# x loaded back beside the edge statistics, and column copies from step 6 to 16 steps before the end, in a graph message-passing kernel on one core

## The chip, the core and the metric

The kernel runs on one core of a Trainium2 chip. Its engines have queues of their own and meet at semaphores: TensorE (PE, weight loads listed as PEld), VectorE (DVE), ScalarE (ACT), GpSimd (POOL) and SyncE (SP), which here issues most of the DMA transfers. The metric is the device time of one execution in microseconds (us). The time before is the median of three runs.

## The reference, cut to what matters

A graph of 12,500 nodes with 96 features and 412,500 directed edges sorted by their target node (a self loop for each node among them). For each edge the rows of x at its source and at its target and a vector made from four edge attributes are joined and put through a linear layer, ReLU and a normalization over all edges (a batch norm); the messages are summed by target node, the nodes' own branch and x are added, and every row is normalized.

```python
def _mlp(h, W, b, gamma, beta):
    h = relu(h @ W + b)
    mu = mean(h, axis=0); var = mean(square(h - mu), axis=0)
    return gamma * (h - mu) * rsqrt(var + EPS) + beta

node_feat = _mlp(x, W_node, ...)
edge_feat = _mlp(edge_attr, W_edge, ...)
message   = _mlp(concat([x[src], x[dst], edge_feat], axis=1), W_msg, ...)
agg       = segment_sum(message, dst, num_segments=12500)
out       = layernorm(x + agg + node_feat)
```

Since the edge features' normalization needs the statistics of all edges, a first pass over the edge attributes comes ahead of the messages.

## The kernel before, in words

**Stages, in order of time.** (1) `tables`: x, transposed, lies in SBUF as `big` (96 partitions, one column of four bytes a node). From it the kernel makes two tables in DRAM, `p_tab` (x times the source part of the message weights) and `q_tab` (the target part). (2) Small things, and `nodes`: the node branch, which overwrites `big` with x plus node branch, and stores that, projected, in `y0_d`. (3) `edge_norm`, the edge statistics: 26 iterations, each with three loads of edge attributes (`ea`, L379), 24 matmuls (L385), 12 ReLUs on ACT (L389) and 24 statistics on DVE (L391). (4) the message stage in `fast`. (5) `output`.

**Gathers.** 412,500 edges are cut into tiles of 128, four tiles make a group (512 edges, 806 groups), four groups a block. For each tile POOL issues an indirect DMA that fetches 128 rows of `p_tab` (L226, `gather`). A ring of seven tiles, each for a pair of groups, holds what was gathered ahead: 14 groups. Since POOL would have nothing to do in stages 1 to 3, the first 116 groups (29 blocks) are gathered then and stored to a DRAM buffer (`spill`, the generator `blocks`, called `store`): each `next(store)` issues 16 gathers on POOL and, on SP, the store of the block two back. They come back 768 KB at a time (`pb`, `fetch`) in the message stage. The first four of these blocks are gathered as raw rows of x before the tables exist, and `convert` multiplies them by the weights in the message stage, group by group, with PE, ACT, PE and DVE in turn.

**The message stage.** `plan` gives an order of the 202 blocks, in which a spilled block follows every five or six others, and from it the steps: one group a step, 806 in all. The order of the instructions of SP, POOL, PE, DVE and ACT is written out by hand (`manual_schedule`). At step k, for group g: every fourth step SP issues the loads of the block two ahead (`load`, `fetch`); `message` on DVE adds the gathered rows to the linear part in PSUM and applies ReLU (L615 for the tiles gathered, L618 and L621 for the fourth tile of some groups); on odd steps ACT squares two groups (L634) and DVE sums squares (L640); `sums` on PE adds up by place (L666); `edges` and `prepare` make the left operand of a coming block (L588, L596); `linear` on PE makes the linear part two steps ahead (L602); and POOL gathers the group 14 ahead (`ahead_of`).

**What relieves POOL.** The fourth tile of some groups isn't gathered. For 40 groups SP fetches its rows one by one, 16 transfers of 384 bytes every second step over 16 steps, with row numbers read into SP's registers (`apart_rows`, `rows_of`, L433); three spilled groups get theirs so in stage 3 (`early_rows`). For others, the *columns*, DVE and ACT copy 128 single columns of x from `big` into a tile `xc` of 96 x 128 (72 copies on DVE, L745, 56 on ACT, L747), from addresses in registers, which are loaded from a small tile of numbers (`clin`, L716, by SP; L733 the register load); `linear` multiplies `xc` by the source weights and adds it to the linear part (L606). Copies are laid out in slots, three in two steps (`XS`); a column takes four slots (`XN`), so 18 copies on DVE and 14 on ACT a slot on average. The slots begin at step `XA`; a column goes to the first group at least four steps after its last slot that has no such help yet and lies ahead of a margin at the end of the stage:

```python
for slot in range(XA // 2 * XS, len(steps) // 2 * XS, XN):
    done = (slot + XN - 1) // XS * 2 + 1
    free = [g for s, g in steps[done + 4:len(steps) - 24] if g >= SPILL and g not in rows and g not in columns]
```

**x for the columns.** Since `nodes` overwrote `big`, x is loaded again, in 14 pieces of 336 KB on SP's queue: `piece`, L697, one on each even step from 2 to 28. After the last copy, `residual` loads `y0_d` into `big` for the output (L453), one load a step from two to three steps past the last slot on.

Of the kernel before, what the change touches and what calls it, by code (L numbers as in the profile page):

```python
# [23 lines left out]
N, C, E, ED = 12500, 96, 412500, 4  # L24
EPS = 1e-5
P = 128
# [16 lines left out]
NB = -(-N // P)  # L43
NN = NB * P
NBK = 4
CH = 14
# [9 lines left out]
SPILL = 29 * BG  # L56
# [12 lines left out]
SR, SS = 16, 2  # L69
SG, SF = 4 * BG, SPILL + 24  # L70
SB = 22
XA, XS, XN = 34, 3, 4
XACT = 56
ROW = 4 * C
FIRST = 16512
# [14 lines left out]
def plan():  # L90

    early, late = list(range(SPILL // BG)), list(range(SPILL // BG, NBL))
    order = []
    for i, b in enumerate(late):
        order.append(b)
        while early and (SPILL // BG - len(early)) * (len(late) - LEAD - SPACE) < (i - LEAD) * (SPILL // BG):
            order.append(early.pop(0))
    assert not early
    steps = [(s, g) for s, b in enumerate(order) for g in range(b * BG, min((b + 1) * BG, NG))]
    at_step = {g: k for k, (s, g) in enumerate(steps)}  # L100
    rows = {g: at_step[g] - SB - at_step[g] % 2 for g in FETCHED[len(EARLY):]}
    columns = {}
    for slot in range(XA // 2 * XS, len(steps) // 2 * XS, XN):
        done = (slot + XN - 1) // XS * 2 + 1
        free = [g for s, g in steps[done + 4:len(steps) - 24] if g >= SPILL and g not in rows and g not in columns]
        if free:
            columns[free[0]] = slot
    return order, steps, rows, columns
# [6 lines left out]
def gnn(ctx, tc, t):  # L115
    nc = tc.nc
    big = ctx.enter_context(tc.tile_pool(name="big", bufs=1)).tile([P, NN], F32, name="big")
# [17 lines left out]
    xp = big[:C]  # L135
    nc.scalar.dma_start(w_msg, t["L0_gnn_W_msg"].rearrange("(s k) f -> k s f", k=C))
    for i in range(0, NB, CH // 2):
        part = slice(i * P, min(i + CH // 2, NB) * P)
# [133 lines left out]
    for i in range(NS):  # L272
        k, n = Q * i, C - Q * i
# [176 lines left out]
    def residual(i):  # L450
# [3 lines left out]
        return y  # L454

    order, steps, by_row, by_column = plan()

    def fast(ring):
# [8 lines left out]
        with tc.manual_schedule(engines={ET.SP, ET.Pool}):  # L467
            nc.sync.dma_start(q_tab[:WM, :], zero[:WM])
            for r in range(WM + NN, WT, 64):
                n = min(64, WT - r)  # L470
                nc.sync.dma_start(q_tab[r:r + n, :], zero[:n])
            for i in range(2):
                next(store)
            places()
            for i in range(3):
                next(store)
            for i, _ in enumerate(nodes()):
                if i in (1, 4, 9):
                    next(store)
            n, extra = 10, early_rows()  # L480
            for i, _ in enumerate(edge_norm()):
                if i:
                    next(extra, None)
                while 14 * i + 180 >= 20 * n:
                    next(store, None)
                    n += 1
            for _ in store:
                pass
            for _ in extra:
                pass  # L490
            got = {g: ahead_of(g) for g in range(SPILL, SPILL + RING)}
        with tc.tile_pool(name="fix", bufs=1) as fix, tc.tile_pool(name="msg", bufs=2) as work, \
# [196 lines left out]
            apart, numbers, held = {}, {}, {}  # L689
            row_start = {k: (i + len(EARLY), g) for i, (g, k) in enumerate(by_row.items())}  # L690
            column_start = {k: g for g, k in by_column.items()}
            pieces = list(range(0, NB, CH // 2))
            loads = list(range(-(-NB // NBY)))

            def piece(i):
                to = slice(i * P, min(i + CH // 2, NB) * P)
                nc.sync.dma_start(big[:C, to], t["xp"][:, to])  # L697

            def apart_rows(k):

# [49 lines left out]
            n, ahead = len(steps), SPILL + RING  # L750
            row_numbers(lin, len(EARLY))
            with tc.manual_schedule(engines={ET.SP, ET.Pool, ET.PE, ET.DVE, ET.Activation}):
                bad = nc.values_load(flag, min_val=0, max_val=1, skip_runtime_bounds_check_because="a comparison's result")
                load(0)
                fetch(0)
                load(1)
                fetch(1)
                for half in range(2):
                    edges(0, half)
                    prepare(0, half)  # L760
                edges(1, 0)
                for k in range(ZB - 1):
                    linear(k)
                places_of(0)
                waiting, last = None, BG * (len(order) - 1)
                for k in range(last):
                    s, g = steps[k]
                    if g % BG == 0:
                        if s + 2 < len(order):
                            load(s + 2)  # L770
                            fetch(s + 2)
                    if k % 2 == 0 and k and pieces:
                        piece(pieces.pop(0))
                    apart_numbers(k)
                    if k % 2 == 0:
                        load_numbers(k, 0, ET.DVE)
                    message(k)
                    load_numbers(k, 1, ET.DVE) if k % 2 else copy_columns(k, 0, ET.DVE)
                    j = k - LATER - BG - 1
                    if k % 2:  # L780
                        load_numbers(k, 1, ET.Activation)
                        copy_columns(k, 1, ET.Activation)
                        now = squared(k - 1)
                        load_numbers(k, 2, ET.Activation)
                        copy_columns(k, 1, ET.DVE)
                        if waiting:
                            moments(waiting, k == last - 1, lambda: load_numbers(k, 2, ET.DVE))
                        waiting = now
                        copy_columns(k, 2, ET.DVE)
                        copy_columns(k, 2, ET.Activation)  # L790
                    if g % BG == 3 and s + 1 < len(order):
                        places_of(s + 1)
                    if j >= 0 and j % BG == 0:
                        add(j // BG, place(j // BG))
                    if k >= LATER:
                        sums(k - LATER)
                    if g % BG != 3 and s + 1 < len(order):
                        if g % 2:
                            edges(s + 1, 1)
                        else:  # L800
                            prepare(s + 1, g % BG // 2)
                    if g % BG == 3:
                        if s + 1 < len(order) and order[s + 1] < RAW:
                            convert(s + 1)
                        if s + 2 < len(order):
                            edges(s + 2, 0)
                    if k + ZB - 1 < n:
                        linear(k + ZB - 1)
                    if k % 2 == 0:
                        load_numbers(k, 0, ET.Activation)  # L810
                        copy_columns(k, 0, ET.Activation)
                    if g >= SPILL:
                        got[ahead] = ahead_of(ahead)
                        ahead += 1
                    apart_rows(k)
                    if k >= (max(column_start) + XN) // XS * 2 + 3 and loads:
                        y0s.append(residual(loads.pop(0)))
                assert not apart and not loads and not pieces

                s, g = len(order) - 1, steps[last][1]  # L820
                m, r = NT - (g + 1) * GT, E - (NT - 1) * P
                collect(waiting.rearrange("p g t c -> p (g t c)"), 2 * GT)
                message(last)
                sq = [squared(last, 1, GT)]
                sums(last - 2)
                sums(last - 1)
                unread(BUSY - 1)
                message(n - 1)
                sq.append(squared(n - 1, 1, m))
                collect(sq[0][:, 0, :, :].rearrange("p t c -> p (t c)"), GT)  # L830
                sums(last)
                at_end = place(s - 1), place(s)
                unread(1)
                collect(sq[1][:, 0, :, :].rearrange("p t c -> p (t c)"), m, r)
                add(s - 1, at_end[0])
                sums(n - 1)
                unread(1)
                square_sum = by_place[s % 2][:C, P:P + 1]
                nc.tensor.matmul(square_sum, squares, ones, start=True, stop=True)
                unread(BUSY)  # L840
                mean_square = fix.tile([C, 1], F32, name="mean_square")
                add(s, at_end[1])
                nc.vector.tensor_scalar(mean_square, square_sum, 1.0 / E, None, op0=OP.mult)
# [236 lines left out]
```

## Time and profile before

| | |
|---|---|
| time, median of 3 runs | 5507.97 us (5506.36 to 5508.45) |
| the profiled execution's own time | 5517.2 us |
| its span | 5515.5 us |
| granted TensorE clock, mean | 0.624 |
| instructions | 97011 |
| edge statistics, first matmul to last statistics | 362.4 to about 942 us |
| first message to last message (806 steps) | 986.9 to 5470.0 us |
| column copies, first to last | 1183 to 5363 us |
| gathers | 2901 |

Rows of groups give the line, the engine and the operation, out<-in by the program's names, the count, then busy time in us and mean ns of one, then the idle time of the engine just before them and what ended most of it. "issue" means that the engine waited for nothing the profile shows. Rows of a timeline give the start, the duration, engine (SPq is SP's queue), line, operation and count, and the idle time before. Rows of stretches give begin and end, length, the busy time and count (x) of the instructions chosen, the granted clock, the share of the DMA engines and GB/s. Rows of waits give who waited for whom: us in total, times, longest. Rows of a line's instructions give shortest, median and longest ns, and the first and last start in us.

### The profile page before, as it was taken

How to read it: one execution, taken by the hardware profiler on the slowest of the kernel's cores; microseconds unless marked ns; L12 is line 12 of the kernel's file. 1: busy time of each engine (PE TensorE's matmuls, PEld its weight loads, DVE VectorE, ACT ScalarE, POOL GpSimd, SP SyncE). 2: the span in 40 equal slices, each digit the busy share in tenths (PEclk: the TensorE clock that was granted, in tenths of full speed). 3: DMA queues.
4: the chain of work that ended last, by engine and by line, in shares of the span. 5: the costliest groups of instructions: out<-in, count | busy, mean ns of one | idle time of the engine just before them, and what ended most of it. 6: DMA issues, size and time to landing. Idle time of an engine off the chain costs nothing. (4 is left out here: it accounts for less than half of the span.)

```text
span 5515.5 us, 97011 instructions
## 1 busy us (share of the span) xinstructions
PE 3422.6 (62%) x17139; PEld 2745.4 (50%) x17139; DVE 3251.4 (59%) x23435; ACT 2835.6 (51%) x16834; POOL 2773.3 (50%) x2930
## 2 busy tenths in 40 slices
PE   3356674666666665666666666666666666666677
PEld 2133332455555555555555555555555555555556
DVE  1436666135556666666666666666666666666664
ACT  0225553135555565565555555555555655565552
POOL 5644445544445545545545545454555554545454
PEclk6555555565666666666666666666666666666657
DMA  6333332211111111111111111111111111111112
GB/s 165 117 89 70 67 75 64 60 51 29 35 33 40 39 37 42 39 38 39 37 40 32 39 39 40 39 38 39 40 40 40 39 39 38 33 39 39 38 49 83
DMA packets 201728, 274.41 MB, mean 50 GB/s; under 512 B 128941, under 2 KB 132166, under 8 KB 200218
## 3 DMA queue, kind: packets, MB, share of 16 engines
q0 software_dynamic: 92832, 142.78, 10.8%
q1 hardware_dynamic: 95304, 120.39, 7.9%
q10 hardware_dynamic: 12960, 4.93, 0.4%
q14 instruction: 494, 4.05, 0.2%
q8 instruction: 138, 2.26, 0.2%
HBM read 221.63 MB, written 46.23 MB: 49 GB/s over the span
## 5 line engine op out<-in xcount | busy, mean ns | idle before, releaser
L226 POOL DMA_INDIRECT pg<-p_tab,src x2837 | 2690.7, 948 | 2634.1 <-DVE h L621 1230.7
L747 ACT ACTIVATE xc<-big 96x4 uint8 x15624 | 1802.8, 192 | 1357.1 <-issue 1337.3
L745 DVE COPY xc<-big 96x4 uint8 x20088 | 1767.7, 185 | 1076.1 <-issue 1047.4
L602 PE MATMUL z<-rhs,left 128*128 128x96 f32 x6446 | 1449.4, 397 | 1392.9 <-remote 1015.3
L602 PEld LDWEIGHTS z<-rhs,left 128*128 128x128 f32 x6446 | 1318.1, 302 | 1784.5 <-remote 1227.1
L666 PE MATMUL pa<-at,h 128*97 128x80 f32 x6446 | 1005.0, 321 | 42.2 <-issue 42.1
L666 PEld LDWEIGHTS pa<-at,h 128*97 128x97 f32 x6446 | 959.5, 242 | 45.8 <-issue 45.7
L615 DVE CUSTOM_DVE_ANT_0 h<-z,pg 128x384 f32<-128x384 f32 (+1 forms) x690 | 348.2, 505 | 340.0 <-remote 130.1
L588 PE MATMUL pr<-ea,we 7*127 7x512 f32 x1380 | 458.5, 744 | 114.7 <-DMA ea<-rel_d 42.5
L596 ACT ACTIVATE left<-pr 127x1024 f32<-127x1024 f32 x403 | 404.4, 1003 | 236.2 <-remote 130.4
L634 ACT ACTIVATE sq<-h 128x768 f32<-128x768 f32 x404 | 339.7, 841 | 360.7 <-DVE h L621 182.4
L385 PE MATMUL pr<-ea,wide 10*128 10x512 f32 x1212 | 393.3, 1072 | 181.2 <-ACT r L389 80.3
L389 ACT ACTIVATE r<-pr 128x1024 f32<-128x1024 f32 x303 | 291.8, 1025 | 405.4 <-remote 185.9
L640 DVE TENSOR_TENSOR mixed<-mixed,sq 128x384 f32<-128x384 f32 x802 | 451.1, 562 | 82.2 <-DVE mixed L640 64.8
L391 DVE BATCH_NORM_STATS2 estats<-r 128x6 f32<-128x512 f32 x606 | 364.5, 678 | 217.1 <-ACT r L389 112.9
L385 PEld LDWEIGHTS pr<-ea,wide 10*128 10x128 f32 x1212 | 196.3, 322 | 376.8 <-issue 209.4
L588 PEld LDWEIGHTS pr<-ea,we 7*127 7x127 f32 x1380 | 118.1, 208 | 156.3 <-issue 71.8
L628 DVE TENSOR_TENSOR at<-rel,mixed 128x496 f32<-128x496 bf16 x202 | 133.9, 663 | 51.7 <-issue 47.8
L606 PE MATMUL z<-w_msg,xc 96*128 96x96 f32 x558 | 162.1, 390 | 0.0
L606 PEld LDWEIGHTS z<-w_msg,xc 96*128 96x128 f32 x558 | 138.2, 303 | 0.0
L226 POOL DMA_INDIRECT pg<-in_x,src_raw x64 | 60.7, 949 | 62.9 <-DMA spill<-pg 42.7
L357 PE MATMUL py<-center,big 96*128 96x96 f32 x196 | 43.7, 424 | 75.7 <-issue 39.4
(126 smaller groups left out, 868.4 us busy)
## 6 DMA issues: line engine op xcount, KB each, us to landing
rowt<-p_tab SPq DMA_DIRECT2D x5120, 0.4 KB
pg<-p_tab,src POOLq DMA_INDIRECT x2837
pb<-spill SPq DMA_DIRECT2D x29, 768.0 KB
spill<-pg SPq DMA_DIRECT2D x55, 384.0 KB
ea<-in_ea SPq DMA_DIRECT2D x75, 160.0 KB
big<-in_xp SPq DMA_DIRECT2D x28, 336.0 KB
rhs<-q_tab SPq DMA_DIRECT2D x202, 46.5 KB
ea<-in_ea SPq DMA_DIRECT2D x228, 30.0 KB
```

Of the source, the lines that this page charges most:

```text
L226: made = [nc.gpsimd.indirect_dma_start(out=pg[:, i, :], out_offset=None, in_=tab[:, :], in_offset=bass.IndirectOffsetOnAxis(ap=idx[:, i:i ...
L385: nc.tensor.matmul(pr[:, k % 2, :], wide[Q * i:Q * i + 2 * EK, :], ea[Q * i:Q * i + 2 * EK, b % J, :], start=True, stop=True)
L391: nc.vector.bn_stats(stats[:, (k - o) % NS, (k - o) // NS, :], r[:, 1 - o, :])
L588: nc.tensor.matmul(prs[s, half][:C + WN, i, :], we[o:o + EK + 2, :], block[s][o:o + EK + 2, :], start=True, stop=True)
L596: nc.scalar.activation(x[:C + WN, 2 * half:2 * half + n, :], pr[:C + WN, :n, :], AF.Relu)
L602: nc.tensor.matmul(zb[k % ZB][:, i * C:(i + 1) * C], left[s % 2][:KR, g % BG, i * P:(i + 1) * P], rhs[:KR, s % RB, g % BG, :], start=True, ...
L615: nc.vector._custom_dve(TENSOR_ADD_SAT, out=h[:, :m, :], in0=z[:, :m, :], in1=got.pop(g)[:, :m, :], s0=MOST, s1=0.0)
L634: nc.scalar.activation(sq[:, :m, :n, :], hb[k // 2 % HP][:, k % 2:k % 2 + m, :n, :C], AF.Square)
L640: nc.vector.tensor_tensor(wide_sq, wide_sq, sq[:, i, :, :], op=OP.add)
L666: nc.tensor.matmul(by_place[s % 2][:C + 1, :NW], hb[k // 2 % HP][:r, k % 2, t, :], at[s % AB][:r, i, o + NW * t:o + NW * (t + 1)], start=i ...
L745: nc.vector.tensor_copy(to, x)
L747: nc.scalar.activation(to, x, AF.Copy)
```

## The change

Three things. x comes back to `big` in the edge statistics: one of the 14 pieces in each of the iterations 2 to 15 of `edge_norm`, on SP's queue behind the rows of that iteration (`early_rows`) and ahead of the spill store, instead of on the even steps 2 to 28 of the message stage. The slots of the column copies begin at step 6 instead of 34. And a column may go to a group up to 16 steps ahead of the stage's end, instead of 24.

```diff
-XA, XS, XN = 34, 3, 4
+XA, XS, XN = 6, 3, 4
...
-        free = [g for s, g in steps[done + 4:len(steps) - 24] if g >= SPILL and g not in rows and g not in columns]
+        free = [g for s, g in steps[done + 4:len(steps) - 16] if g >= SPILL and g not in rows and g not in columns]
...
-            n, extra = 10, early_rows()
+            n, extra, pieces = 10, early_rows(), range(0, NB, CH // 2)
             for i, _ in enumerate(edge_norm()):
                 if i:
                     next(extra, None)
+                if 2 <= i < 2 + len(pieces):
+                    part = slice(pieces[i - 2] * P, min(pieces[i - 2] + CH // 2, NB) * P)
+                    nc.sync.dma_start(big[:C, part], t["xp"][:, part])
                 while 14 * i + 180 >= 20 * n:
                     next(store, None)
                     n += 1
...
-            pieces = list(range(0, NB, CH // 2))
             loads = list(range(-(-NB // NBY)))
-
-            def piece(i):
-                to = slice(i * P, min(i + CH // 2, NB) * P)
-                nc.sync.dma_start(big[:C, to], t["xp"][:, to])
...
-                    if k % 2 == 0 and k and pieces:
-                        piece(pieces.pop(0))
                     apart_numbers(k)
```

More of the change, by code (lines that the diff above doesn't have):

```diff
@@ L817, in fast @@
                         y0s.append(residual(loads.pop(0)))
-                assert not apart and not loads and not pieces
+                assert not apart and not loads
                 s, g = len(order) - 1, steps[last][1]
```

## The prediction

> **What bounds the kernel now.** I read the page first, for the engines and the costliest groups, then stretches of the trace by stage and by step, then the instructions of single queues.
>
> ```profile
> span 5515.5 us, 97011 instructions
> ...
> PE 3422.6 (62%) x17139; PEld 2745.4 (50%) x17139; DVE 3251.4 (59%) x23435; ACT 2835.6 (51%) x16834; POOL 2773.3 (50%) x2930
> ...
> L226 POOL DMA_INDIRECT pg<-p_tab,src x2837 | 2690.7, 948 | 2634.1 <-DVE h L621 1230.7
> L747 ACT ACTIVATE xc<-big 96x4 uint8 x15624 | 1802.8, 192 | 1357.1 <-issue 1337.3
> L745 DVE COPY xc<-big 96x4 uint8 x20088 | 1767.7, 185 | 1076.1 <-issue 1047.4
> ```
>
> No engine is full. POOL, which issues the gathers, mostly waits for DVE: its ring of 14 groups is full, and it goes on when a message frees a pair (1230.7 us of its idle time). So the gathers are not short on the whole. DVE and ACT spend most of their instructions on column copies (20088 / 72 = 15624 / 56 = 279 columns), and their idle time there, 1047.4 and 1337.3 us, is "issue": they wait for nothing that the profile names. A DVE timeline shows what that is.
>
> ```profile
> 2526.12 0.17 DVE L745 COPY xc<-big 96x4 uint8 x1 [0.55 <-issue]
> 2526.83 0.17 DVE L745 COPY xc<-big 96x4 uint8 x1 [0.54 <-issue]
> 2527.54 0.59 DVE L745 COPY xc<-big 96x4 uint8 x7 [0.54 <-issue]
> ```
>
> A copy comes every 0.71 us, and then, all at once, seven in 0.59 us, that is (0.59 - 0.17) / 6 = 0.07 us apart. So there are slow spells in which an instruction costs ten times its price. They belong to POOL's bursts. The queue of SP in the edge statistics shows it, with the same 16 row transfers issued twice:
>
> ```profile
> 427.72 9.70 SPq L433 DMA_DIRECT2D erow<-p_tab  x16
> 437.54 0.83 SPq L253 DMA_DIRECT2D spill<-pg  x2
> 441.21 1.05 SPq L379 DMA_DIRECT2D ea<-in_ea  x3
> 443.65 19.52 SPq L433 DMA_DIRECT2D erow<-p_tab  x16
> 463.20 0.36 SPq L253 DMA_DIRECT2D spill<-pg  x1
> 463.65 0.38 SPq L250 DMA_DIRECT2D spill<-pg  x1
> 464.12 0.43 SPq L251 DMA_DIRECT2D spill<-pg  x1
> 466.49 1.05 SPq L379 DMA_DIRECT2D ea<-in_ea  x3
> ```
>
> 9.70 us where POOL rests, 19.52 us where it issues a block of 16 gathers. How dense the gathers come is in these stretches of L226 (us, POOL busy, count):
>
> ```profile
> 989.40:1125.50 136.10, 88.90 (x94) 0.61 0.25 66
> 2408.40:2420.40 12.00, 6.62 (x7) 0.64 0.13 30
> 1013.00:1036.60 23.60, 15.13 (x16) 0.64 0.19 51
> ```
>
> At the start of the message stage, without copies, 16 gathers run in one burst and the next begins 23.6 us later; with copies, a burst has seven and 12.0 us pass. One gather takes 0.948 us (the page's mean) and an issue of 764.1 / 2501 = 0.306 us after it, 1.25 in all:
>
> ```profile
> POOL pg L226 <- issue: 764.1, 2501, 0.6
> ```
>
> So the message stage is bound by a balance: DVE, ACT and PE work in the time that POOL's bursts leave them, and POOL waits for them. A column takes one gather out of a burst and puts 72 DVE and 56 ACT copies in. The pace by steps is one message (L615) a step:
>
> ```profile
> 986.80:1145.20 158.40, 13.15 (x24) 0.60 0.23 62
> 1145.20:1157.80 12.60, 2.22 (x4) 0.71 0.13 36
> 1157.80:1286.20 128.40, 10.48 (x20) 0.64 0.17 43
> 1302.80:1459.40 156.60, 12.04 (x24) 0.61 0.15 37
> 1459.40:1475.90 16.50, 2.22 (x4) 0.78 0.02 5
> 1475.90:1608.40 132.50, 10.03 (x20) 0.63 0.15 37
> 986.80:1013.70 26.90, 3.35 (x6) 0.50 0.22 58
> 1302.80:1336.50 33.70, 2.92 (x6) 0.65 0.15 36
> 2068.70:2209.40 140.70, 12.14 (x24) 0.64 0.16 42
> 5352.20:5396.00 43.80, 3.94 (x8) 0.50 0.23 63
> ```
>
> The first three rows are steps 0 to 23, 24 to 27 (a spilled block, which needs no gather) and 28 to 47; copies begin at step 34. The next three are the same kinds of steps one turn later (52 to 75, 76 to 79, 80 to 99), all with copies. Each of the 24s and 20s holds one conversion of a raw block.
>
> **How much changes.** From the plan: slots went 51, 55, ... before, 9, 13, ... after, up to 1208; the end of the stage leaves the last 11 slots without a group before and the last 8 after. So 290 - 11 = 279 columns become 300 - 8 = 292: ten or eleven more in steps 6 to 33, two or three more after step 777. That is 13 gathers of 1.25 us less on POOL, 13 x 72 DVE copies and 13 x 56 ACT copies more, 13 small loads of numbers more on SP, and for each column two short matmuls and one DVE operation in place of a part of another. Between, every slot carries as many copies as it did (the slots shift by 42, an even count, and shares alternate by two); the columns fall on steps four later in a pattern of eight, which is one block. I count the middle at nothing, give or take 3 us.
>
> **Start of the message stage.** Price it by the stretches with copies. Steps 0 to 23: 156.6 - 158.4 = -1.8. Steps 24 to 27: 16.5 - 12.6 = +3.9, since copies now stand in line between the conversion and the messages. Steps 28 to 47: 132.5 - 128.4 = +4.1. Sum +6.2 us. Against it, the first six steps still have no copies and took 26.9, not 33.7: -6.8, as far as POOL lets that lead last. So -0.6 to +6.2. The farthest end below: if POOL alone paced this stretch, ten gathers less would be -12.5 us (94 gathers took 94 x 1.25 = 117.5 of its 136.1 us), and the 14 pieces of x that leave SP's queue would add at most
>
> ```profile
> L697 SPq DMA_DIRECT2D big<-in_xp x14: 328/562/2502, 979.3 to 1157.5; - x14
> ```
>
> 14 x 0.56 = 7.8 us, together -20. I take +1: the stretches with copies are the nearest row, and POOL rests between its bursts with them.
>
> The Trainium skill (SBUF — State Buffer, "Who interferes with whom") states that only the port pair shared by DVE and GpSimd causes contention, so that PE, ACT and SP would lose nothing to gathers. By that rule fewer gathers would give those engines nothing, the start would go by +6 and the sum come to 5514. The trace does not agree: SP's 16 transfers went from 9.70 to 19.52 us beside a burst.
>
> **Edge statistics.** Fourteen pieces of 336 KB now stand in SP's queue, one an iteration, behind the 16 rows and ahead of the spill store and the loads of `ea`. Nothing in this stage uses x. Behind a piece wait the store, for which POOL waits before its next 16 gathers, and the loads, for which PE waits an iteration later.
>
> ```profile
> 466.35 0.95 POOL L226 DMA_INDIRECT pg<-p_tab,src  x1 [6.02 <-DMA spill<-pg]
> ```
>
> ```profile
> SPq L379 <- PE pr L385: 53.2, 18, 7.1
> ```
>
> POOL went on 1.8 us after SP had issued its last store (464.12 + 0.43 to 466.35). I take that as an estimate of what a piece of similar size holds the store back, with the 0.56 us of its issue 2.4 us. SP has 53.2 / 18 = 3.0 us to spare where it waits for PE before it loads: the cover. POOL's burst begins up to 2.4 us later, but PE then has as much more of the fast time ahead of the slow spell. Bounds 0 and, if each iteration with a store grew by the whole 2.4 us (some ten of the fourteen, my estimate from SP's queue), +24. I take +1. If the cover went (more than 3 us a piece), SP would be late next.
>
> **End of the stage.** Copies now run to about step 784, not 777. The eight steps 776 to 783 took 43.8 us; at the pace with copies (140.7 / 24 = 5.86) they would take 46.9: +3.1. Three gathers fewer before the last are -3.75, and the end hangs on POOL as its last gather starts only 20.8 us ahead of the last message:
>
> ```profile
> L615 DVE CUSTOM_DVE_ANT_0 h<-z,pg x690: 445/547/560, 986.9 to 5470.0; 128x384 f32<-128x384 f32 x112, 128x288 f32<-128x288 f32 x61
> ```
>
> ```profile
> L226 POOL DMA_INDIRECT pg<-p_tab,src x2837: 942/947/3990, 125.7 to 5449.2; - x190
> ```
>
> Together -0.7; bounds -4 and +3, I take -1. The 13 loads of the residual start at step 787 instead of 781, one a step, so the last is issued at step 799, still ahead of the output: nothing.
>
> **Sum.** +1 + 1 - 1 = +1 us. The profiled execution took 5517.2 us (its span 5515.5), 9.2 above the median of the runs, 5508.0; by it the sum is 5518.2, and on the scale of the median 5509.
>
> **The rivals.** *POOL paces the start and the end.* Then the 13 gathers are worth their whole price, 16.3 us: 5492, and 5484 if SP's relief counts too. For it: 94 gathers fill 86% of 136.1 us. Against it: over a whole turn (steps 0 to 47 against 52 to 99) the stretches with copies are no shorter, 299.4 against 305.6 us.
>
> *The pieces hold up POOL in the edge statistics*, the other side. A piece in front of the spill store delays every burst, the slow spell ends later by that much, SP's rows, which wait in that spell (19.52 us of 25), end later, and so do the next store and load. Price: ten iterations of 2.4 us, +24: 5532. It decides once a piece costs SP more than the 3.0 us to spare. For it: back-to-back blocks leave POOL only some 6 us of rest (6.02 above). Against it: SP does wait for PE in most iterations.
>
> The Trainium skill (DMA: Bandwidth & Descriptors, "Queues, rings and completion order") speaks for this rival: on each DMA engine descriptors of one queue are consumed in ring order, so a store does queue behind a piece. The 1.8 us of the row is consistent with it; no run here shows the two back to back.
>
> *DVE and ACT become the bound at the start*: copies that fall into slow spells cost 0.71 us each, and the conversion's ping-pong between PE, ACT and DVE waits behind them. Price: +6.2 for the first turn without the lead, and as much again if the loads of numbers come late behind SP's rows: +12, 5520. That the copies do not begin early at all is ruled out by the plan, which gives a group for slot 9.
>
> **How the numbers follow.** My forecast 0.45, its own range 5497 to 5519 (0.2% of 5508 is 11 us, about what a measurement of this kernel can tell from no change). POOL pacing 0.25. The pieces 0.2, copies as the bound 0.1. So faster 0.25, same 0.45, slower 0.3. The range, 5488 to 5532, takes in the middle of the rival below (5492) and the price of the one above (5532), and leaves out the far end of the first (5484) and anything beyond the second.
>
> **What would show it.** Right: in the stretches of L615, steps 0 to 23 within 5 us of 157, 24 to 27 near 16.5, the edge statistics' last BATCH_NORM_STATS2 within 5 us of where it was, 2888 gathers in all, bursts of seven from step 10 on, and the last message some 20 us behind the last gather. The first rival: steps 0 to 27 shorter by over 10 us with POOL's rests near zero. The second: SP's waits for PE in L379 gone, and the whole message stage shifted late by over 10 us at unchanged pace. Wrong altogether: a middle whose 24 steps differ from 140.7 by more than 1 us on the mean, for then the place of the columns matters, which I count at nothing.

## The result and the profile after

The kernel after takes 5516.4 us (median of 22 runs, 5501 to 5535) where the kernel before, run beside it, takes 5509.8 (22 runs, 5500 to 5546). The ratio is 1.0002, 95% interval [0.999, 1.0014], which is +1 us with -5.5 and +7.7 as its ends. (The two medians alone would give 1.0012, which lies inside that interval too.) The forecast was 5509, "same", with a sum of +1 us. So the sum holds, within an interval 13 us wide; whether its terms do is another question, and most of what follows is about them.

The profile page of the kernel after, its span and the three groups that the change moves:

```profile
span 5503.8 us, 98862 instructions
...
L226 POOL DMA_INDIRECT pg<-p_tab,src x2824 | 2677.6, 948 | 2634.1 <-DVE h L624 1277.2
L745 ACT ACTIVATE xc<-big 96x4 uint8 x16352 | 1880.3, 192 | 1420.3 <-issue 1404.8
L743 DVE COPY xc<-big 96x4 uint8 x21024 | 1853.3, 185 | 1146.6 <-issue 1121.0
```

21024 / 72 = 292 columns in place of 279, and 13 gathers less (2824 and 64 of the raw rows, 2888). POOL is busy 13.1 us less in its group and idle for 2634.1 us ahead of it, as before to the tenth. The copies' idle time that waits for nothing has grown with their count.

The message stage of the kernel after, one message (L618, which was L615) a step. The stretches are those of the prediction: steps 0 to 23, 24 to 27, 28 to 47; then 80 to 103, 104 to 439, 440 to 775, 776 to 783 and 784 to the last message. The first numbers are the stretch and its length in us:

```profile
981.77:1135.34 153.57, 12.76 (x24) 0.64 0.15 37
1135.34:1151.79 16.45, 2.22 (x4) 0.83 0.02 6
1151.79:1280.67 128.88, 9.93 (x20) 0.60 0.16 40
1470.58:1616.37 145.79, 12.25 (x24) 0.66 0.14 36
1616.37:3480.64 1864.27, 170.70 (x336) 0.64 0.15 39
3480.64:5339.85 1859.21, 170.92 (x336) 0.64 0.15 38
5339.85:5387.60 47.75, 4.12 (x8) 0.50 0.15 38
5387.60:5459.86 72.26, 11.21 (x21) 0.70 0.31 96
```

Those of the kernel before that the prediction doesn't show, from step 80 on:

```profile
1475.98:1626.79 150.81, 12.26 (x24) 0.63 0.13 34
1626.79:3493.06 1866.27, 170.91 (x336) 0.65 0.15 39
3493.06:5352.32 1859.26, 170.79 (x336) 0.64 0.15 38
5352.32:5396.06 43.74, 3.94 (x8) 0.50 0.23 64
5396.06:5469.97 73.91, 11.51 (x21) 0.71 0.26 79
```

The first 24 steps are 4.9 us shorter, the spilled block is 3.9 us longer, as forecast to the tenth, and steps 28 to 47 are 0.4 longer. Together 298.9 us against 299.4. The middle is 2.1 us shorter over 672 steps, and the 29 steps of the end 2.4 us longer. Of the 11.7 us between the two spans, 5.0 come from steps 80 to 103, where nothing changed, and 5.1 from the edge statistics; runs of one kernel differ by more than that, so it is no gain. Of the other signs that the prediction named, the gathers are 2888, POOL's bursts have 6 to 8 gathers from step 9 on, where seven were forecast from step 10, and POOL still rests between them.

### The profile page after: what moved, and what is told of

Read it like the earlier page. It is cut to its first block, busy times and chain, and to the rows that moved or that the text cites. A ratio compares the mean times of both kernels' runs of the same rounds, so it can differ in the third digit from the quotient of the medians.

```text
span 5503.8 us, 98862 instructions
## 1 busy us (share of the span) xinstructions
PE 3433.9 (62%) x17165; PEld 2763.4 (50%) x17165; DVE 3333.4 (61%) x24384; ACT 2910.7 (53%) x17562; POOL 2760.3 (50%) x2917
## 5 line engine op out<-in xcount | busy, mean ns | idle before, releaser
L226 POOL DMA_INDIRECT pg<-p_tab,src x2824 | 2677.6, 948 | 2634.1 <-DVE h L624 1277.2
L745 ACT ACTIVATE xc<-big 96x4 uint8 x16352 | 1880.3, 192 | 1420.3 <-issue 1404.8
L743 DVE COPY xc<-big 96x4 uint8 x21024 | 1853.3, 185 | 1146.6 <-issue 1121.0
L618 DVE CUSTOM_DVE_ANT_0 h<-z,pg 128x384 f32<-128x384 f32 (+1 forms) x690 | 347.1, 503 | 213.8 <-issue 114.2
L226 POOL DMA_INDIRECT pg<-in_x,src_raw x64 | 60.8, 949 | 63.8 <-DMA spill<-pg 43.6
```

The costliest lines, as they stand in the source:

```text
L226: made = [nc.gpsimd.indirect_dma_start(out=pg[:, i, :], out_offset=None, in_=tab[:, :], in_offset=bass.IndirectOffsetOnAxis(ap=idx[:, i:i ...
L618: nc.vector._custom_dve(TENSOR_ADD_SAT, out=h[:, :m, :], in0=z[:, :m, :], in1=got.pop(g)[:, :m, :], s0=MOST, s1=0.0)
L743: nc.vector.tensor_copy(to, x)
L745: nc.scalar.activation(to, x, AF.Copy)
```

## The experiments

They ran on several chips, and these fall in two groups. On some the kernel before takes 5508 to 5584 us and shows the slow spells of the prediction; on two others the same kernel takes 3739 us and shows none. Each ratio is against the kernel before on the same chip. The result above is from a chip of the first group.

### One part at a time, on chips with slow spells

**Pieces alone.** The kernel after with the plan of before, so that of the three changes only the moved loads of x remain:

```diff
-XA, XS, XN = 6, 3, 4
+XA, XS, XN = 34, 3, 4
...
-        free = [g for s, g in steps[done + 4:len(steps) - 16] ...
+        free = [g for s, g in steps[done + 4:len(steps) - 24] ...
```

> Only the 14 pieces of x are moved to the edge statistics; the copies begin at step 34 and end 24 steps ahead as before. The balance (my theory, edits hidden): the same time as before within 0.2% (11 us), the edge statistics no longer by more than 3 us, the first 24 steps at 154 to 159 us. The rival that pieces hold up POOL's bursts: 20 to 25 us more than before, all of it ahead of the first message.

It took 5579.7 us where before took 5584.0, ratio 0.9993 [0.997, 1.0016]. It ran again later, on a chip where before takes 5508.

> The pieces alone once more: the kernel after with the copies of columns from step 34 and to 24 steps ahead of the end, so only the 14 pieces of x stand beside the edge statistics. On a chip with slow spells it took 0.9993 of before. On a chip without them the kernel after has its first message at 647.6 us, against 642.9 in the kernel with late columns, whose edge statistics are those of before. If the pieces hold SP up and POOL's one unbroken row of gathers is not touched, the first message again comes some 5 us late, and the time is 1.0000 (POOL makes the end) to 1.0013 (+5 us) there. If the 11.5 us that the whole change costs there are the pieces': 1.003.

There it took 5510.3, ratio 0.9996 [0.998, 1.0012]. Steps 0 to 23, 24 to 27 and 28 to 47 of this second run:

```profile
985.04:1142.53 157.49, 13.22 (x24) 0.65 0.18 39
1142.53:1158.00 15.47, 2.22 (x4) 0.50 0.02 4
1158.00:1289.19 131.19, 10.49 (x20) 0.60 0.18 39
```

The edge statistics don't grow: the first message comes at 985.0 us (986.9 before). But the three stretches sum to 304.1 us, and 305.5 in the first run, where the three profiles that have the pieces in the message stage and no early copies give 299.4, 300.3 and 298.6. So the message stage begins some 5 us slower with the pieces moved, in both runs. No theory on record had that. Of the 5 us, 3.0 lie in the spilled block, in the third and the fourth of its messages, and go with the clock that TensorE was granted (the number behind the count). From the third to the fourth, in the kernel before and with the pieces alone:

```profile
1152.60:1155.42 2.82, 0.56 (x1) 1.00 0.01 1
```

```profile
1149.80:1155.04 5.24, 0.56 (x1) 0.50 0.00 2
```

DVE waits there for PE, and the same eight matmuls of `linear` that take 1.13 us in the kernel before take 2.02 us with the pieces alone. In the other profiles with the loads of x in the message stage (the end alone, twice) the clock is 1.00 there too, and with the pieces alone it is 0.50 both times. Why the clock rises later with the pieces moved no run shows.

The edge statistics take the pieces in without growing because SP had time to spare. SP's waits for PE before it loads `ea` (L379), 53.2 us in the kernel before and 54.1 with no loads of x at all (the third kernel below), are 38.9 and 40.3 us with the pieces alone, and in the kernel after:

```profile
SPq L379 <- PE pr L385: 31.3, 10, 6.1
```

**The end alone.** The kernel before, with columns up to 16 steps ahead of the end:

```diff
-        free = [g for s, g in steps[done + 4:len(steps) - 24] ...
+        free = [g for s, g in steps[done + 4:len(steps) - 16] ...
```

> Only the margin at the end is changed, 16 instead of 24; copies begin at step 34 and the pieces stay in the message stage. The balance: within 4 us of before, steps 776 to 783 at about 47 us (43.8 before), given back by step 805. POOL as the bound at the end: 4 us or more less.

It took 5585.4 us, ratio 1.0012 [0.9993, 1.0032]; and again later:

> The end alone once more: the kernel before with copies up to 16 steps ahead of the end in place of 24, three columns more. On a chip with slow spells it took 1.0012 of before [0.9993, 1.0032]. On a chip without them POOL issues its last gather 2.8 us ahead of the last message, so that POOL makes the end and three gathers of 1.25 us less are worth -3.75 us, 0.999. If the copies in the last 24 steps hold the messages up there: 1.001 to 1.003, and the last message comes later behind the last gather. What then is left of the +11.5 us of the whole change belongs to the columns at steps 6 to 33: ten gathers less, -12.5 us, against POOL's rests of 14.6, 15.8 and 19.8 us in the steps 52 to 131, which the kernel with columns from step 154 on doesn't have.

5518.1 us, ratio 1.0004 [0.9985, 1.0023]. Of that run, steps 776 to 783 and 784 to the last message:

```profile
5359.25:5407.23 47.98, 4.12 (x8) 0.57 0.18 38
5407.23:5488.43 81.20, 11.12 (x21) 0.67 0.29 85
```

Sum 129.2 us, and 131.1 in the first of the two runs, 120.0 in the kernel after, 127.2 in the next kernel, which also has the late copies. With the margin of 24 the same 29 steps take 117.7 (before), 118.7 and 123.4 (pieces alone). On the mean 126.9 against 119.9: in single profiles the late columns cost the end some 7 us (2.4 from before to after, 12.4 between the first runs of the end alone and the pieces alone on one chip), though up to three gathers are gone.

**Without the pieces.** The kernel after with the 14 loads of x left out:

```diff
-                if 2 <= i < 2 + len(pieces):
-                    part = slice(pieces[i - 2] * P, min(pieces[i - 2] + CH // 2, NB) * P)
-                    nc.sync.dma_start(big[:C, part], t["xp"][:, part])
```

> The changed kernel with the 14 loads of x left out altogether, so that the copies read what the node branch left in that tile; same copies, same steps. The balance: as the changed kernel within 0.2%. The rival that pieces hold up POOL: 20 to 25 us less than the changed kernel.

5582.0 us, ratio 0.999 [0.9967, 1.0012]. Its first message comes at 985.4 us and its steps 0 to 47 take 302.6. The kernel leaves out x, so its copies read what the node branch left in `big`. In the edge statistics the pieces cost nothing that can be measured: the rival that had them hold up POOL for 24 us falls on these chips.

**No columns at all.** The kernel before with no group given to a column, so every tile is gathered; the residual starts at step 781 as before:

```diff
+    columns = {}
     return order, steps, rows, columns
...
-                    if k >= (max(column_start) + XN) // XS * 2 + 3 and loads:
+                    if k >= 781 and loads:
```

> The kernel before with no columns at all: 279 gathers more, 20088 DVE and 15624 ACT copies less. POOL paces (the gather has its whole price): 279 x 1.25 = 349 us more. DVE and ACT pace (the copies have theirs): at least 279 x 72 x 0.07 = 1406 us less of DVE work, so some hundred us less. The balance, in which a gather out and a column's copies in cancel: within 2% of before (110 us), with bursts of 16 gathers, 24 gathered steps at about 143 us (before: 140.7) and the four steps of a spilled block at about 12.5 us (before: 16).

5803.7 us, ratio 1.038 [1.0332, 1.0428], +212 us. That is 212 / 279 = 0.76 us a column: not the 1.25 us of POOL pacing, and about twice the 110 us in all that a mere balance was given. The gathers of its page, and steps 52 to 75, 76 to 79, 80 to 103, 104 to 439 and 440 to 775:

```profile
L227 POOL DMA_INDIRECT pg<-p_tab,src x3116 | 2946.7, 946 | 2652.7 <-DVE h L616 1480.7
```

```profile
1308.99:1471.56 162.57, 12.89 (x24) 0.60 0.18 39
1471.56:1483.51 11.95, 2.22 (x4) 0.75 0.02 4
1483.51:1633.75 150.24, 12.95 (x24) 0.64 0.17 37
1633.75:3634.64 2000.89, 181.66 (x336) 0.62 0.18 38
3634.64:5633.15 1998.51, 181.50 (x336) 0.62 0.18 39
```

279 gathers more made POOL 256 us busier and left its idle time as it was (2652.7 against 2634.1 us): it still stands mostly waiting for messages with its ring full. (With the end alone, on the chip of this run, the idle time is 2708.0 us.) So POOL doesn't pace; that the other engines pay for the gathers, in the slow spells, fits this, but the kernel also lost all its copies, so their two prices aren't told apart. The chip was 1 to 2% slower than that of the result, so the stretches are set against the end alone on the same chip, whose middle is that of before. Its steps 104 to 439 and 440 to 775:

```profile
1641.88:3540.18 1898.30, 170.72 (x336) 0.65 0.17 38
3540.18:5414.93 1874.75, 170.83 (x336) 0.64 0.17 38
```

In these 672 steps the columns, some 250, are worth 3999.4 - 3773.1 = 226 us, 0.9 each. A spilled block, which needs no gather, loses by them (11.95 us without, 16.44 with). And ahead of step 104 they are worth little: steps 28 to 51 take 150.4 us without and 145.1 with, steps 52 to 103 324.8 and 323.6, which is 6.4 us for the 26 columns of steps 34 to 103. The change puts its ten new columns still further ahead.

### The same kernels on chips without slow spells

**The kernel after, again.**

> The kernel after itself, beside the kernel before. On one chip the kernel before takes some 5510 to 5580 us, with slow spells beside POOL's bursts; on another it takes 3739, without them, and there POOL issues gathers one after the other through nearly the whole span. On a chip with slow spells, if a column at the start is worth little: 1.000 within 0.002. If it is worth the mean of 0.76 us: -10 us, 0.998. On a chip without them, if POOL paces all of it: 13 gathers of 1.24 us less are -16 us, 0.9957; at the 0.46 us a column that the 45 late columns cost there (+20.6 us): -6 us, 0.998.

3749.7 us where before took 3739.7, ratio 1.0031 [1.0012, 1.005]: there the change is 11.5 us slower, which no forecast had. The same groups of the page as above, for the same kernel, instruction for instruction:

```profile
span 3750.7 us, 98862 instructions
...
L226 POOL DMA_INDIRECT pg<-p_tab,src x2824 | 2674.7, 947 | 926.7 <-issue 789.9
L743 DVE COPY xc<-big 96x4 uint8 x21024 | 1670.8, 193 | 92.8 <-issue 84.6
L745 ACT ACTIVATE xc<-big 96x4 uint8 x16352 | 1654.9, 191 | 58.5 <-issue 46.1
```

A gather takes the same 947 ns, but the copies' idle time is 92.8 us in place of 1146.6 on DVE and 58.5 in place of 1420.3 on ACT. SP's row transfers show the same. First, 16 of them beside POOL's resting and 16 beside a burst, in the kernel after on a chip with slow spells, and POOL's gathers in those two stretches:

```profile
429.13 8.51 SPq L433 DMA_DIRECT2D erow<-p_tab  x16
...
445.07 19.04 SPq L433 DMA_DIRECT2D erow<-p_tab  x16
```

```profile
429.13:437.64 8.51, 0.00 (x0) 0.50 0.18 24
445.07:464.11 19.04, 13.24 (x14) 0.50 0.29 52
```

And on the chip without them, where POOL issues 19 gathers in the 22.4 us:

```profile
307.45 9.22 SPq L433 DMA_DIRECT2D erow<-p_tab  x16
...
319.63 10.26 SPq L433 DMA_DIRECT2D erow<-p_tab  x16
```

```profile
307.45:329.89 22.44, 16.95 (x19) 0.50 0.56 92
```

**Columns late.** The kernel before with 45 columns fewer, all at the start of the message stage:

```diff
-XA, XS, XN = 34, 3, 4
+XA, XS, XN = 154, 3, 4
```

> The kernel before, with the copies of columns beginning at step 154 in place of 34: 45 columns fewer, all at the start of the message stage. If an early column is worth what a column is worth on the mean (212 us / 279 = 0.76 us): +34 us, 1.006, the steps 28 to 160 longer by that. If early columns are worth nothing, as the ten at steps 6 to 33 seem to be: 1.000 within its interval.

3748.8 us, ratio 1.0055 [1.0032, 1.0078], +20.6 us; 45 gathers are 45 x 1.25 = 56 us of POOL. Its steps up to 34 have no copies, as those of before; no profile of before was taken on such a chip, so this one stands for it. Steps 0 to 33 and 776 to the last message, with columns late:

```profile
642.84:755.10 112.26, 18.79 (x34) 0.79 0.39 93
3576.27:3698.82 122.55, 15.62 (x29) 0.59 0.32 82
```

and in the kernel after on the chip without slow spells:

```profile
647.59:781.75 134.16, 17.78 (x34) 0.78 0.24 55
3602.05:3689.01 86.96, 15.44 (x29) 0.80 0.37 102
```

With early copies the first message comes 4.7 us later and the first 34 steps take 21.9 us more (the pieces are moved too, and are not told apart here). The steps between differ by 0.9 us in all, and the last 29 take 35.6 us less, but little of that is left in the whole: POOL's gathers, from the row of L226, run to 3696.1 us with columns late and to 3686.3 with the kernel after, 9.8 us less for 58 gathers less (58 x 1.25 = 72.5 us). The waits of POOL in the kernel after say where the rest went:

```profile
POOL pg L226 <- DVE h L624: 63.9, 25, 20.1
```

With columns late the row for h after L621 has 4.6 us, 15 times, 0.3 at the most: POOL never rests for a message. In the kernel after it rests with its ring full, three times above all, for 14.6, 15.8 and 19.8 us (at 854, 975 and 1078 us, worked out from the starts of the gathers, without the 0.3 us of issue). The first of them ends here in POOL's timeline:

```profile
868.81 0.95 POOL L226 DMA_INDIRECT pg<-p_tab,src  x1 [14.86 <-DVE h L624]
```

All rests over 0.5 us sum to 63.5 us in the kernel after and to 4.9 with columns late, so 58.6 of the 72.5 us that the gathers set free became rests. That says why the early columns gain little over columns late. Why the kernel after is slower there than before stays open: the second runs of the pieces alone and of the end alone, meant to split the 11.5 us, fell on a chip with slow spells.

**No copies.** The kernel before with the fourth tile of the 279 column groups neither gathered nor copied:

```diff
-                                     ... stop=g not in by_column or i < GT - 1)
-                if g in by_column:
-                    nc.tensor.matmul(zb[k % ZB][:, (GT - 1) * C:GT * C], apart.pop(g), w_msg[:, 0, :], ...
+                                     ... stop=True)
...
-                for g, slot in by_column.items():
+                for g, slot in ():
```

> The kernel before, with its 279 columns neither gathered nor copied: the fourth tile of those groups gets neither a gather nor the 128 copies of DVE and ACT, nor the two short matmuls, nor the loads of numbers; that part of the messages is left out. Without columns, every tile gathered, the time was 1.038 of before (+212 us). If the gathers alone set the pace (POOL paces): 279 x 1.25 = 349 us below that kernel, so 137 us below before, 0.975. If the copies alone set it (DVE and ACT pace, 279 x 128 copies of some 0.07 to 0.1 us on two engines, about 5.5 us a column on each): copies gone give more than 349, down to some 0.92 of before. If what counts is the number of instructions that fall into the slow spells of the bursts: both matter, and the time lies between, some 0.95.

3705.6 us, ratio 0.9901 [0.9869, 0.9933], -37 us. The +212 us of the kernel without columns belong to the other chips, so the two can't be set against each other, and the price of the copies in slow spells stays open. Here the reading is plain: DVE's busy time is halved (1563.4 us against 3099.5 in the kernel after, both on such chips) and 1% of the time goes, because POOL's gathers, 2901 x 1.25 = 3626 us, fill the span of 3703.8: in its message stage POOL never pauses for more than 0.3 us between two of them.

**Spaced gathers and short bursts.** Two edits of the kernel after that were meant to take the slow spells away:

```diff
+            nc.gpsimd.memset(rest, 0.0)          # behind every gather
```

> The kernel after, with a memset of 128 x 64 f32 on POOL behind every gather, so that gathers follow each other at a lower rate. If the slow spells come from gathers issued back to back (a burst must be 4 to 6 us old before other engines slow down), they become rarer or milder: copies on DVE closer to 0.1 than to 0.7 us apart in a burst, and the time falls, by up to 3 per cent. If each gather costs the others a fixed amount, however spaced, or if POOL paces: 2888 memsets of an estimated 0.1 to 0.3 us more on POOL, no change to +0.6 ms x the share in which POOL paces, that is 1.00 to 1.05.

```diff
-    ring = rpool.enter_context(tc.tile_pool(name="ring", bufs=RING // 2))
+    ring = rpool.enter_context(tc.tile_pool(name="ring", bufs=RING))
...
-                for i in range(0, BG, 2):
-                    pg = ring.tile([P, 2, GT, C], F32, name="pg")
...
+                for i in range(BG):
+                    pg = ring.tile([P, GT, C], F32, name="pg")
```

> The kernel after, with the ring of gathered rows cut into 14 tiles of one group instead of 7 of a pair, so that POOL goes on as soon as one message has freed a group: in the message stage bursts of three or four gathers in place of seven; the spill stores go group by group too. If only bursts older than 4 to 6 us slow the other engines, the slow spells nearly go and the time falls by 1 to 4 per cent. If each gather costs the others a fixed amount, wherever it is: no change, 0.995 to 1.005. If the additional stores on SP and the finer waits cost: up to 1.01.

> The kernel after with the ring cut into 14 tiles of one group (as short bursts before, where the chip had no slow spells and it took 1.0037 of before). On a chip with slow spells: if only bursts older than 4 to 6 us slow the other engines, bursts of three or four gathers end before that and the time falls by 1 to 4 per cent. If each gather costs the others a fixed amount: 0.995 to 1.005. On a chip without slow spells: 1.002 to 1.006 again, since POOL is seldom held up by the ring and SP has more stores to issue.

All three fell on chips without slow spells, so they say nothing of them. Spacing took 1.0245 [1.0222, 1.0267], +92 us. A memset takes 169 ns, but most of it falls into the 0.3 us of issue between two gathers: their starts follow each other 1.28 us apart in place of 1.25 (medians). That is 0.03 us a gather, 2888 x 0.03 = 87 us where POOL sets the pace. So the edit hardly spaced the gathers, and would hardly have tested the slow spells on another chip either. Short bursts took 1.0037 [1.0019, 1.0054] and 1.0019 [0.9998, 1.0039], no different from the kernel after itself there (1.0031). Whether shorter bursts help on a chip with slow spells is not tried. No kernel that computes the whole ran faster than before beyond its interval, on either group of chips.

## Why the prediction was right, point by point

That the measured ratio stands at +1 us, as the sum did, is in part luck: the interval is 13 us wide, and where +1, +1 and -1 us were forecast for start, edge statistics and end, the profiles of before and after show -0.5, -5.0 and +2.4, of which the second lies within what single profiles scatter. What the runs bear out is the mechanism behind a forecast of "same": POOL does not pace, and gathers taken off it at the start are worth little. The parts below are read from single profiles. None of the parts run alone moved the whole time beyond its interval (pieces 0.9993 and 0.9996, end 1.0012 and 1.0004).

**Start of the message stage, +1 us.** Measured -0.5 (298.9 against 299.4 for steps 0 to 47), and the parts compensate in another way than the sum had it. The spilled block's +3.9 came exactly. The relief of SP by the pieces, bounded at -7.8 to 0, has the wrong sign: the pieces alone make these steps 4.7 to 6.1 us longer. Some 3 us of that go with TensorE's clock in the spilled block, a term that the sum did not have. The columns alone are then worth 298.9 - 304.8 = -5.9 (304.8 being the mean of the two runs with the pieces alone); set against the prediction's stretches with copies, the +4.1 of steps 28 to 47 was not there (+0.4). Without pieces at all the sum was 302.6, so each of these terms is known to some 3 us.

**Edge statistics, +1 us.** Right on chips with slow spells. The last BATCH_NORM_STATS2 starts at

```profile
L391 DVE BATCH_NORM_STATS2 estats<-r x606: 673/676/695, 368.6 to 936.5; 128x6 f32<-128x512 f32 x152
```

where it was 941.5, and at 941.1 and 939.9 with the pieces alone. The -5.0 is not a gain: with the end alone, whose edge statistics are those of before, it is 955.9 and 956.8, and the time is the same (the executions profiled were 7 and 16 us above the medians of their runs). The cause of that swing of 15 us isn't known. The cover that the prediction named is in the traces: SP's waits for PE fell from 53.2 to 31.3 us and did not end. On the chips without slow spells the cover was smaller and is used up, and the pieces do cost what the rival had in kind though not in size: 596.8 us with columns late, 602.2 in the kernel after, +5.4. SP's waits there, with columns late and in the kernel after:

```profile
SPq L379 <- PE pr L385: 24.9, 19, 2.7
```

```profile
SPq L379 <- PE pr L385: 5.7, 11, 2.3
```

**End, -1 us.** This is the term that was mis-sized. Steps 776 to 783 took +4.0 (forecast +3.1; +6.0 and +4.2 with the end alone), but the -3.75 of three gathers came only in part in the kernel after (-1.7 from step 784 on) and not with the end alone (+7.4 and +7.3): the four profiles with late copies need 126.9 us on the mean from step 776 on, against 119.9 for the three without. The last gather went before the last message by 22.9 us, as forecast, and 32.5 and 32.6 with the end alone. The prediction took such a gap as a sign that POOL sets the end. The trace of before says otherwise: POOL rests with its ring full until a message frees a pair, twice from step 784 on, the second time until 28 us ahead of the last message:

```profile
5441.71 0.95 POOL L226 DMA_INDIRECT pg<-p_tab,src  x1 [3.89 <-DVE h L615]
```

So the messages, not the gathers, are late there. Where POOL does not rest, on the chips without slow spells, its last gather goes 2.8 us ahead of the last message.

**Middle, 0 +- 3 us.** Right: -2.0 and -0.1 over 336 steps each, and 24 steps differ from before by under 0.2 us on the mean.

**The balance.** On chips with slow spells POOL has its 2634 us of idle time with and without the change, and 279 gathers more left it there while the time rose by 212 us. That fits a gather that costs by what it does to the others, and a column is worth 0.76 us on the mean, 0.9 in the middle and a quarter of one at the first turn. Thirteen at the mean would be -10 us. Of it the start's columns show 5.9; the moved pieces (+5 beside the messages) and the end (+7, or +2.4 in the one profile of the kernel after) take it back. With +7 these sum to +6, with +2.4 to +2, both inside the measured interval.

**The rivals.** *POOL paces* falls here (0.76 us a column, not 1.25; idle time unchanged). On the chips without slow spells it describes the middle, where POOL issues without a break, and yet the change is slower there: three times in the first 110 steps messages, not gathers, are the slower side, and POOL waits for them with a full ring. *The pieces hold up POOL*: not on these chips; 5.4 us on the others. *Copies the bound at the start* is the rival that comes nearest to what those other chips do (steps 0 to 33 longer by 21.9 us); here the first 48 steps stayed as long as they were.

## What to carry to other kernels

Where one engine fills a ring ahead of its users and does not disturb them, as on the chips without slow spells, work taken off it is worth something only in stretches where the users wait for it; ask of each stretch who rests, and don't put the exchange where the ring is full. Where its work slows its users, as on the other chips, taking work off it can pay even while it rests (0.9 us a column in the middle). Where a large mean price (212 us for 279 columns) is measured, look at it by stretch before buying more of the same: here nearly all of it lay in the middle. And a time that depends on how engines disturb each other belongs to the chip it was measured on: measure on more than one before tuning against it.

## What the runs showed of the hardware that was not expected

The same program takes 5516 us on one chip and 3750 on another, with gathers of the same 947 ns. The difference that the traces show is that on the first other engines issue slowly beside POOL's bursts. From the starts of DVE's copies that follow each other directly, in the kernel before, on the mean: 0.07 us apart in the first three us of a burst, 0.12 in the fourth, 0.48 in the fifth, 0.54 in the sixth, 0.68 in the seventh and after; 0.66 in the first us behind the burst and 0.08 in the next. On the chip without slow spells they stay 0.07 us apart. TensorE's clock is not what makes it, at least in the edge statistics: there it was granted 0.50 on both, and the stage took 538 us from its first matmul to its last in the kernel after on the one chip and 364 on the other. What is different about the chips is not known. The Trainium skill (SBUF — State Buffer, "Who interferes with whom") has only the port pair of DVE and GpSimd contend. On the chips without slow spells SP's transfers agree with it (9.22 and 10.26 us for 16 transfers beside 19 gathers); on the others something slows SP that this rule does not name (8.51 and 19.04). Whether SBUF has a part in it no run shows.

The last row of matmuls, 196 of them with no others beside, ran at the full clock in one profile and at half in another, both on chips without slow spells. With columns late, and then in the kernel after, the time in us and, behind the count, the granted clock:

```profile
3707.81:3729.93 22.12, 22.12 (x196) 1.00 0.46 123
```

```profile
3698.28:3740.41 42.13, 42.12 (x196) 0.50 0.31 85
```

The same 196 matmuls cost 20 us more at half the clock, nearly twice the whole effect of the change on such a chip. Of the six profiles from such chips five have half the clock there and columns late alone the full one; all eight from the others have the full one. What decides it no run shows; it is why the two spans (3746.2 and 3750.7 us) stand the other way round than the last gathers (3696.1 and 3686.3). The times of single executions there lie in two groups 15 to 20 us apart (columns late 3747 to 3749 and 3766 to 3768, before on that chip 3721 to 3728 and 3737 to 3750), and set group against group columns late costs 22 to 26 us rather than 20.6. That the clock of the last row makes the groups is likely but not shown.
